# One PSUM pool for the whole program, exponential's table taken up early, and the first query copies on VectorE, in a perceiver layer on one core

## The chip, the cores and the metric

The kernel runs on one core of a Trainium2 chip. It is one launch. The metric is the time of the device in microseconds (us), the median of several runs. All data are float32. The engines are TensorE (PE), VectorE (DVE), ScalarE (ACT), GpSimd (POOL) and SyncE (SP), which here issues the loads and stores. Matrix products are written to PSUM, which has eight banks of 128 partitions by 512 float32 values; VectorE and ScalarE read them from there.

## What is computed

One layer of a perceiver with 256 query tokens of 512 channels and 25088 context tokens: cross attention with a sigmoid instead of a softmax, causal self-attention of 16 heads with one set of keys and values, and a mixture of 64 experts, 8 to a token, with a shared expert.

```python
def xattn(q, k, v, ...):                       # 256 x 512, 25088 x 512
    qp, kp, vp = q @ Wq.T + bq, k @ Wk.T + bk, v @ Wv.T + bv
    return sigmoid(qp @ kp.T / sqrt(128)) @ vp

def attn(x, ...):
    xn = layernorm(x, ln_g, ln_b)
    q, (k, v) = xn @ w_q.T, split(xn @ w_kv.T)       # 16 heads of 64; one k, one v
    p = softmax(causal(q * scale @ k.T))
    return layernorm((p @ v, all heads) @ w_out.T, lno_g, lno_b)

def ffn(x, ...):
    shared = (silu(g) * u) @ s_down * sigmoid(x @ shared_gate_w)
    w, idx = top_k(softmax(x @ gate_w), 8)           # of 64 experts
    return sum over the 8 of w * ((silu(g_e) * u_e) @ e_down) + shared

x = x + xattn(layernorm(x), context, context)
x = x + attn(layernorm(x))
x = x + ffn(layernorm(x))
```

## The kernel before

The program is one function, `tile_perceiver_layer`. `T` is 256 tokens in `NT` = 2 tiles of `P` = 128, `D` is 512 channels in `ND` = 4 chunks. Tiles of memory come from pools; a scheduler places the waits. An instruction waits for earlier users of the tiles that it touches, and a new tile in a used buffer waits for the readers of the old one. When a pool is closed and another takes its place, a tile in that place waits for the last users of the old pool there. Many instructions are given to `in_turn`, which keeps the written order among the instructions of an engine; the gate, up and down matmuls of the shared part and the experts (L899 to L965) are mostly not, so the scheduler moves them.

The cross stage (L448 to L485) goes over 49 groups of 512 context tokens. For each group the context is transposed, keys `pk` and scores `pz` are made, and the sigmoids `zT` are multiplied with the context. This last product is made by seven products of half size ("00", "01", "2", "3", "1", "4", "11", L427 to L446), which are added up in PSUM over all groups: they lie in four banks, `held` (L389), two products to a bank, from the pool `pacc`. The other four banks, the pool `psum`, are handed out in turn by `bank`. After the last group eight VectorE instructions (L491 to L498) combine the products to `zc`, which is transposed (`pt_zc`), multiplied with the value weights (`py`, L530) and normed (`an`, L541). The first tile of `an` is transposed during the second `py` (L539): ScalarE copies four chunks out of PSUM into `anT`.

Then `cross.close()` gives both pools back (L543) and the pool `psum_b` takes all eight banks (L545): one bank each for the tags `pa`, `po`, `pt0`, `pt1`, and two pairs for the scores (`ps2`). The self-attention's heads are worked on in `NE` = 8 pairs. For each pair: `queries` (four matmuls, L624, and a copy `aq` by ScalarE, L633), `scored` (L702: four matmuls, then VectorE adds the mask and takes the maxima), `exponential` (L731, ScalarE), `divided` (L745: VectorE's reciprocals, then POOL's product), `turned` (transposes `ptp` and copies `pT`) and `weighted` (`po`, L784). The loop (L798) staggers these: a round makes the scores of pair e, and turns the probabilities of pair e − 2; `queries` runs one or two pairs ahead. Queries of pairs 1 and 3 take the bank `po`, the others `pa`. Before the loop stand keys, values and queries of pair 0, in halves, as the tiles of `anT` come.

The output projection (`project`, L683) adds up `pw_0` and `pw_1` over the pairs. Some of its matmuls are fillers (L696) that the last rounds put between the others. `attended` norms the result, adds the residual (`x2`) and norms it again (`fn`).

At L852 the heads' pool is closed, and `pacc_b` (two banks) and `psum_c` (six banks) open. `route` (L863) makes the router's logits `pl`, `gate_up_products` the first shared products in two banks `first` (L931), before and after the second tile of `fn` is transposed. `run` (L967) then goes over four parts of the shared expert and eight whole experts: `gate_up` (two banks `ph`), and one step later `down` (L944), which makes the two token tiles `pd` one after the other in the two banks of `pacc_b`, each followed by VectorE's addition to `y` (L959, L963). Seven experts with few tokens are done by `few_*`, gathered in rounds; `few_spread` (L1213) adds them to `y` by `pd_few` in the banks of `pacc_b` too. SP loads each expert's weights (`load_expert`) when a buffer of the pool `wpool`, of three, is free.

Of the kernel before, what the change touches and what calls it, by code (L numbers as in the profile page):

```python
# [9 lines left out]
F32 = mybir.dt.float32  # L10
AF = mybir.ActivationFunctionType
ALU = mybir.AluOpType
AX = mybir.AxisListType

P = 128
# [6 lines left out]
def tile_perceiver_layer(  # L22
# [25 lines left out]
    nc = tc.nc  # L48

    T, D = x.shape  # L50
# [9 lines left out]
    ND = D // P  # L60
# [11 lines left out]

    cross = ExitStack()
    cpool = cross.enter_context(tc.tile_pool(name="cpool", bufs=2))
    psum = cross.enter_context(tc.tile_pool(name="psum", bufs=4, space=bass.MemoryType.PSUM))
    pacc = cross.enter_context(tc.tile_pool(name="pacc", bufs=4, space=bass.MemoryType.PSUM))

    def bank(name):
        return psum.tile([P, 512], F32, tag="ps", name=name)

    def accbank(name):
        return pacc.tile([P, 512], F32, tag="acc", name=name)

# [169 lines left out]
        in_turn(nc.vector.reciprocal(rs, sd))  # L255
        in_turn(nc.vector.tensor_scalar(dst, src, mean, rs, ALU.subtract, ALU.mult))

    def transposed_tile(dst, src, t, nm, by_act, g=None, b=None, psum_of=None):


        pt = bank(f"pt_{nm}_{t}") if psum_of is None else psum_of(f"pt_{nm}_{t}")
        for c in range(ND):
            in_turn(
                nc.tensor.transpose(
                    pt[:, c * P : (c + 1) * P], src[:, t, c * P : (c + 1) * P], ident
                )
            )
        pc = pt.rearrange("p (c q) -> p c q", c=ND)
        to = dst[:, :, t * P : (t + 1) * P]
        if g is None:  # L270
            if by_act > 0:
                in_turn(nc.scalar.copy(to[:, 0:by_act, :], pc[:, 0:by_act, :]))
            if by_act < ND:
                in_turn(nc.vector.tensor_copy(to[:, by_act:ND, :], pc[:, by_act:ND, :]))
            return
        for c in range(ND):
            if c < by_act:
                in_turn(
                    nc.scalar.activation(
                        to[:, c, :], pc[:, c, :], AF.Identity, bias=b[:, c : c + 1],  # L280
                        scale=g[:, c : c + 1],
                    )
                )
            else:
                in_turn(
                    nc.vector.tensor_scalar(
                        to[:, c, :], pc[:, c, :], g[:, c : c + 1], b[:, c : c + 1],
                        ALU.mult, ALU.add,
                    )
                )  # L290
# [95 lines left out]

    NP = J // 2
    HD = D // 2
    held = [accbank(f"xacc_{i}") for i in range(4)]  # L389
    product = {  # L390
        nm: held[i // 2][:, (i % 2) * HD : (i % 2 + 1) * HD]
        for i, nm in enumerate(("00", "01", "2", "3", "1", "4", "11"))
# [133 lines left out]
    for t in range(NT):  # L526
# [14 lines left out]
        layernorm(an[:, t, :], x1[:, t, :], f"a{t}", twice=True)  # L541

    cross.close()  # L543
    heads_psum = ExitStack()
    psum = heads_psum.enter_context(  # L545
        tc.tile_pool(name="psum_b", bufs=1, space=bass.MemoryType.PSUM)
    )

    def head_bank(tag, name):
        return psum.tile([P, 512], F32, tag=tag, name=name)  # L550

    def score_banks(name):
        return psum.tile([P, 2, 512], F32, tag="ps2", name=name, bufs=2)

# [57 lines left out]
    kk = hpool.tile([P, T], F32, tag="kk", name="kk")  # L616
    va = hpool.tile([P, NT, DH], F32, tag="va", name="va")

    def queries(e, lo=0, hi=T, tag="pa", mark=lambda ins: ins):

        pa = head_bank(tag, f"pa_{e}_{lo}")
        for c in range(ND):
            mark(
                nc.tensor.matmul(  # L624
                    pa[:, 0 : hi - lo],
                    lhsT=a_wqT_sb[:, c, e * P : (e + 1) * P],
                    rhs=anT[:, c, lo:hi],
                    start=(c == 0),
                    stop=(c == ND - 1),
                )  # L630
            )
        in_turn(
            nc.scalar.activation(aq[:, e, lo:hi], pa[:, 0 : hi - lo], AF.Copy, scale=1.0 / DH)  # L633
        )

    def head_keys(lo, hi):
        pkk = head_bank("po", f"pkk_{lo}")
        for c in range(ND):
            in_turn(
                nc.tensor.matmul(  # L640
                    pkk[:, 0 : hi - lo],
                    lhsT=a_wkv_sb[:, c, 0:2, :].rearrange("p i d -> p (i d)"),
                    rhs=anT[:, c, lo:hi],
                    start=(c == 0),
                    stop=(c == ND - 1),
                )
            )
        nc.scalar.copy(kk[:, lo:hi], pkk[:, 0 : hi - lo])

    def head_values(t):  # L650
        pv = head_bank("pt1", f"pv_{t}")
        for c in range(ND):
            in_turn(
                nc.tensor.matmul(
                    pv[:, :DH],
                    lhsT=anT[:, c, t * P : (t + 1) * P],
                    rhs=a_wkv_sb[:, c, 2, :],
                    start=(c == 0),
                    stop=(c == ND - 1),
                )  # L660
            )
        in_turn(nc.vector.tensor_copy(va[:, t, :], pv[:, :DH]))


    first_scores = score_banks("ps_0")
    head_keys(0, P)
    queries(0, 0, P, mark=in_turn)
    transposed_tile(
        anT, an, 1, "an", 2, ln_g_sb, ln_b_sb, lambda name: head_bank("pt0", name)
    )  # L670
    head_values(0)
    head_keys(P, T)
    queries(0, P, T, mark=in_turn)
    head_values(1)


# [5 lines left out]

    def project(t, e):  # L683
        if len(pw) == t:
            pw.append(head_bank("pa", "pw_0") if t == 0 else score_banks("pw_1")[:, 0, :])
        in_turn(
            nc.tensor.matmul(  # L687
                pw[t],
                lhsT=oT[:, e, t * P : (t + 1) * P],
                rhs=a_wout_sb[:, e, :],  # L690
                start=(e == 0),
                stop=(e == NE - 1),
            )
        )

    fillers = [(0, e) for e in range(NE - 1)] + [(1, 0)]  # L696

    def fill(n):
        for _ in range(n):
            project(*fillers.pop(0))  # L700

    def scored(e):  # L702

        ps = first_scores if e == 0 else score_banks(f"ps_{e}")
        parts = []
        for t in range(NT):
            nk = (t + 1) * P
# [44 lines left out]
    def turned(e):  # L752


        found = [pe for pe, _ in scores_of.pop(e)[2]]
        done = []
        for kt in range(NT):
            pt = head_bank(f"pt{kt}", f"ptp_{e}_{kt}")
            n = (NT - kt) * P
            for i in range(2):  # L760
                for t in range(kt, NT):
                    o = i * n + (t - kt) * P
                    in_turn(
                        nc.tensor.transpose(
                            pt[:, o : o + P], found[t][:, i, kt * P : (kt + 1) * P], ident
                        )
                    )
            pT = work_b.tile([P, 2, n], F32, tag=f"pT{kt}", name=f"pT_{e}_{kt}")
            to = pT.rearrange("p i q -> p (i q)")
            if kt == 0:  # L770
                in_turn(nc.vector.tensor_copy(to, pt[:, : 2 * n]))
            else:
                in_turn(nc.scalar.copy(to, pt[:, : 2 * n]))
            done.append(pT)
        return done

    def weighted(e, done):


        po = head_bank("po", f"po_{e}")  # L780
        for kt, pT in enumerate(done):
            for i in range(2):
                in_turn(
# [10 lines left out]


    scores_of = {}
    queries(1, tag="po", mark=in_turn)
    for e in range(NE + 2):  # L798
        done = None
        if e == 2:  # L800
            queries(e + 2, mark=in_turn)
        if e - 2 in scores_of:
            done = turned(e - 2)
        if e - 1 in scores_of:
            divided(e - 1, 0)
            divided(e - 1, 1)
        if e == 1:
            queries(e + 1, mark=in_turn)
        if e != 2 and 0 < e < NE - 2:
            queries(e + 2, tag="po" if e == 1 else "pa", mark=in_turn)  # L810
        if e >= NE - 2:
            fill(2 if e < NE else 1)
        if e < NE:
            scores_of[e] = scored(e)
        if done is not None:
# [26 lines left out]
    fill(len(fillers))  # L842
    project(0, NE - 1)
    attended(0)
    for e in range(1, NE):
        if e == NE - 1:
            transposed_tile(fT, fn, 0, "fn", ND, psum_of=lambda name: head_bank("pt0", name))
        project(1, e)
    attended(1)

    heads_end.close()
    heads_psum.close()  # L852
    pacc = ctx.enter_context(tc.tile_pool(name="pacc_b", bufs=2, space=bass.MemoryType.PSUM))
    psum = ctx.enter_context(tc.tile_pool(name="psum_c", bufs=6, space=bass.MemoryType.PSUM))
    few = ctx.enter_context(tc.tile_pool(name="few", bufs=1))


# [3 lines left out]
    pls = []  # L861

    def route(t):  # L863
        pl = bank(f"pl_{t}")
        for c in range(ND):
            in_turn(
                nc.tensor.matmul(
# [60 lines left out]

    first = [bank(f"ph_first_{half}") for half in range(2)]  # L931
    route(0)
    gate_up_products(("s", 0), first, 0, P, in_turn)
    transposed_tile(fT, fn, 1, "fn", 2)
# [9 lines left out]
    def down(n, hT):  # L944
        _, dn = weights.pop(n)
        nm = f"{n[0]}{n[1]}"
        for t in range(NT):
            pd = accbank(f"pd_{nm}_{t}")
            for f in range(NI):
                nc.tensor.matmul(  # L950
                    pd,
# [259 lines left out]
        nc.scalar.copy(of_sb[:, r, :], po)  # L1211

    def few_spread():  # L1213
        for t in range(NT):
            pd = accbank(f"pd_few_{t}")
            for r in range(NR):
                nc.tensor.matmul(  # L1217
                    pd,
# [126 lines left out]
```

## Time and profile before

| | us |
|---|---|
| median of 3 runs | 803.3 (802.87 to 804.76) |
| the profiled execution | 804.36 |
| its span | 802.6 |
| TensorE busy | 786.0 (98%) |
| VectorE busy | 496.0 (62%) |
| ScalarE busy | 112.3 (14%) |
| POOL busy | 19.3 (2%) |

The span runs from the first to the last instruction that the profile shows; the time of the execution has a little more around it. The page shows the span in 40 slices of 20 us. In tenths, 9 being 90% or more:

```profile
PE   8999999999999999999999999999999899999996
...
DVE  5766777667776677667776677766546453512212
ACT  2111100111011110111101110011145220110110
...
PEclk9999999999999999999999999999999999999999
DMA  9997999999999888988889888910600032769500
```

The cross stage ends at about 565 us, the heads run to about 640 us, the shared part and the experts to the end. The rows of DMA give the mean share of 16 DMA engines; PEclk is the clock that TensorE was granted, in tenths of the full one, as a mean of the slice.

### The profile page before, as it was taken

What the parts mean: (1) busy time and instruction counts of PE and PEld (TensorE: products, weight loads), DVE (VectorE), ACT (ScalarE), POOL (GpSimd) and SP (SyncE); (2) the same over time, 40 slices, a digit from 0 to 9 for tenths busy, and PEclk for the clock granted to TensorE, in tenths of its full rate; (3) what the DMA queues carried; (4) which work ended last, traced back from release to release, by engine and by line L of the source; (5) the groups of instructions that cost most, each with busy time, mean ns of one, the idle gap of its engine ahead of it and who ended that gap; (6) DMA issues with size and microseconds to landing.
All of it is one profiled execution on the core that took longest, in us unless ns stands there. A gap on an engine that the chain in (4) does not pass through costs nothing.

```text
span 802.6 us, 8728 instructions
## 1 busy us (share of the span) xinstructions
PE 786.0 (98%) x3310; PEld 565.8 (70%) x3310; DVE 496.0 (62%) x819; ACT 112.3 (14%) x248; POOL 19.3 (2%) x42
## 2 busy tenths in 40 slices
PE   8999999999999999999999999999999899999996
PEld 5777777777777777777777777777675576776563
DVE  5766777667776677667776677766546453512212
ACT  2111100111011110111101110011145220110110
POOL 1000000000000000000000000000123000000000
PEclk9999999999999999999999999999999999999999
DMA  9997999999999888988889888910600032769500
GB/s 251 242 198 182 266 237 256 241 228 227 216 205 197 188 180 176 203 189 192 177 179 207 187 188 171 190 53 0 228 10 1 1 131 83 249 222 386 187 1 30
DMA packets 150496, 139.59 MB, mean 174 GB/s; under 512 B 7984, under 2 KB 109872, under 8 KB 150448
## 3 DMA queue, kind: packets, MB, share of 16 engines
q1 hardware_dynamic: 150160, 138.96, 73.7%
q8 instruction: 28, 0.46, 0.3%
q14 instruction: 20, 0.16, 0.1%
q10 hardware_dynamic: 288, 0.00, 0.0%
HBM read 138.42 MB, written 0.52 MB: 173 GB/s over the span
## 4 chain that ended last, share of the span: by engine, by line
PE 95%; DVE 2%; ACT 1%; POOL 1%; DMA 0%; issue 0%; ACTq 0%; POOLq 0%; DVEq 0%
PE xacc L439 37%; PE pk L338 21%; PE pz L360 11%; PE ph_e L904 7%; PE pd_e L950 3%; PE ph_s L904 3%; PE pd_s L950 2%; PE pw L687 2%; PE pa L624 1%; PE ph_few L1172 1%; PE py L530 1%; PE ph_first L904 1%; PE po_few L1203 1%; PE ps L713 1%; PE pf L1149 1%; PE pd_few L1217 1%
## 5 line engine op out<-in xcount | busy, mean ns | idle before, releaser
L338 PE MATMUL pk<-cT,wkT_sb 128*128 128x512 f32 x376 | 169.0, 592 | 0.0
L439 PE MATMUL xacc<-T,S 128*128 128x256 f32 x588 | 134.9, 379 | 0.0
L368 ACT ACTIVATE zT<-pz 128x512 f32<-128x512 f32 x98 | 58.3, 597 | 479.9 <-PE pz L360 479.2
L439 PEld LDWEIGHTS xacc<-T,S 128*128 128x128 f32 x588 | 111.7, 190 | 15.2
L338 PEld LDWEIGHTS pk<-cT,wkT_sb 128*128 128x128 f32 x376 | 71.4, 190 | 69.9 <-issue 67.4
L309 DVE STREAM_TRANSPOSE cT<-quarters 128x2048 f32<-128x2048 f32 x47 | 108.2, 2303 | 0.0
L439 PEld LDWEIGHTS xacc<-ctx,zT 128*128 128x128 f32 x392 | 74.3, 190 | 31.3 <-issue 23.0
L439 PE MATMUL xacc<-ctx,zT 128*128 128x256 f32 x392 | 93.0, 380 | 0.1
L360 PE MATMUL pz<-qT,kT 128*128 128x256 f32 x392 | 92.6, 379 | 0.0
L360 PEld LDWEIGHTS pz<-qT,kT 128*128 128x128 f32 x392 | 74.4, 190 | 10.1
L407 DVE TENSOR_TENSOR S<-zT 128x256 f32<-128x256 f32 x49 | 20.8, 425 | 91.5 <-ACT zT L368 91.5
L347 DVE TENSOR_SCALAR kT<-pk,bk 128x512 f32<-128x512 f32 x49 | 36.8, 751 | 59.8 <-PE pk L338 59.8
L904 PE MATMUL ph_e<-fT,gu 128*128 128x256 f32 x256 | 57.2, 381 | 0.0
L380 DVE TENSOR_TENSOR zsum<-zsum,zT 128x1024 f32<-128x1024 f32 x48 | 56.8, 1182 | 0.0
L904 PEld LDWEIGHTS ph_e<-fT,gu 128*128 128x128 f32 x256 | 48.1, 190 | 10.6 <-issue 3.8
L439 PE MATMUL xacc<-T,zT 128*128 128x256 f32 x196 | 50.3, 379 | 0.0
L439 PE MATMUL xacc<-ctx,S 128*128 128x256 f32 x196 | 50.3, 379 | 0.0
L439 PEld LDWEIGHTS xacc<-T,zT 128*128 128x128 f32 x196 | 37.2, 190 | 5.1
L439 PEld LDWEIGHTS xacc<-ctx,S 128*128 128x128 f32 x196 | 37.2, 190 | 5.1
L418 DVE TENSOR_TENSOR T<-ctx,T 128x512 f32<-128x512 f32 x49 | 33.9, 692 | 1.7
L419 DVE TENSOR_TENSOR T<-ctx 128x512 f32<-128x512 f32 x49 | 33.5, 684 | 0.0
L420 DVE TENSOR_TENSOR T<-T,ctx 128x512 f32<-128x512 f32 x49 | 33.5, 683 | 0.0
(225 smaller groups left out, 611.3 us busy)
## 6 DMA issues: line engine op xcount, KB each, us to landing
ctx<-in_context SPq DMA_DIRECT2D x48, 1024.0 KB, 7.5
quarters<-in_context SPq DMA_DIRECT2D x188, 256.0 KB, 9.3
gu<-in_e_gate_up SPq DMA_DIRECT2D x12, 1024.0 KB, 7.8
dn<-in_e_down SPq DMA_DIRECT2D x11, 512.0 KB, 5.5
gu_s<-in_s_gate_up SPq DMA_DIRECT2D x8, 512.0 KB, 6.6
a_wqT<-in_a_wqT SPq DMA_DIRECT2D x1, 2048.0 KB, 9.0
a_wout<-in_a_woutT SPq DMA_DIRECT2D x1, 2048.0 KB, 9.0
dn_s<-in_s_down SPq DMA_DIRECT2D x4, 512.0 KB, 8.3
```

The source lines that it names most:

```text
L309: in_turn(nc.vector.transpose(cT, q.rearrange("p b (c r) -> p c b r", r=R)))
L338: nc.tensor.matmul(pk, lhsT=w[:, c, :], rhs=cT[:, c, :, :].rearrange("p b r -> p (b r)"), start=(c == 0), stop=(c == ND - 1),)
L347: in_turn(nc.vector.tensor_scalar(kT, pk, bk_sb, None, ALU.add))
L360: nc.tensor.matmul(pz[:, i * T : (i + 1) * T], lhsT=kT[:, j * P : (j + 1) * P], rhs=qT, start=True, stop=True,)
L368: nc.scalar.activation(zT[:, 2 * h : 2 * h + 2, :].rearrange("p j t -> p (j t)"), pz, AF.Sigmoid, scale=1.0 / math.sqrt(QK),)
L380: in_turn(nc.vector.tensor_add(zsum, zsum, zT))
L418: in_turn(nc.vector.tensor_sub(t2, c_of(ct, 1, 1), t1))
L419: in_turn(nc.vector.tensor_sub(t3, c_of(ct, 1, 1), c_of(ct, 0, 1)))
L420: in_turn(nc.vector.tensor_sub(t4, t2, c_of(ct, 1, 0)))
L439: nc.tensor.matmul(product[nm], lhsT=lhs[:, p, :], rhs=rhs[:, p, :], start=(g == 0 and p == 0 and nm in ("00", "2", "1", "11")), stop=(g = ...
L904: nc.tensor.matmul(ph[:, f * T + lo : f * T + hi], lhsT=gu[:, c, col : col + P], rhs=fT[:, c, lo:hi], start=(c == 0), stop=(c == ND - 1),)
L950: nc.tensor.matmul(pd, lhsT=hT[:, f, t * P : (t + 1) * P], rhs=dn[:, f, :], start=(f == 0), stop=(f == NI - 1),)
```

## The change

All three pools become one, `psum`, open from the start to the end, with eight banks: three of a tag "one", one of a tag "apart", and two pairs of a tag "two", each pair one tile.

- `bank` takes in turn three tiles of "one" and one of "apart".
- `held` is cut from two pairs. So are `first`, both halves of each `pd` and of `pd_few`, the scores `ps` and `pw_1`.
- `pkk`, `pv`, `ptp`, `po`, the transposes and `pl` take "one"; all `queries` and `pw_0` take "apart".
- A small exponential, `warm`, is put on ScalarE between the transposes of the second tile of `an` and the second values and keys.
- The copies `aq` of pairs 1 to 3 are made by VectorE, the others as before by ScalarE.
- There is one more filler, (1, 1), and the last round takes two of them.

```diff
-    psum = cross.enter_context(tc.tile_pool(name="psum", bufs=4, space=bass.MemoryType.PSUM))
-    pacc = cross.enter_context(tc.tile_pool(name="pacc", bufs=4, space=bass.MemoryType.PSUM))
+    psum = ctx.enter_context(tc.tile_pool(name="psum", bufs=3, space=bass.MemoryType.PSUM))
+    turns = [0]
 
     def bank(name):
-        return psum.tile([P, 512], F32, tag="ps", name=name)
-
-    def accbank(name):
-        return pacc.tile([P, 512], F32, tag="acc", name=name)
+        turns[0] += 1
+        return apart(name) if turns[0] % 4 == 0 else among_three(name)
+
+    def among_three(name):
+        return psum.tile([P, 512], F32, tag="one", name=name)
+
+    def apart(name):
+        return psum.tile([P, 512], F32, tag="apart", name=name, bufs=1)
+
+    def banks(name):
+        return psum.tile([P, 2, 512], F32, tag="two", name=name, bufs=2)
...
-    held = [accbank(f"xacc_{i}") for i in range(4)]
+    held = [pair[:, i, :] for pair in (banks("xacc_0"), banks("xacc_1")) for i in range(2)]
...
-    heads_psum = ExitStack()
-    psum = heads_psum.enter_context(
-        tc.tile_pool(name="psum_b", bufs=1, space=bass.MemoryType.PSUM)
-    )
...
-    def queries(e, lo=0, hi=T, tag="pa", mark=lambda ins: ins):
-
-        pa = head_bank(tag, f"pa_{e}_{lo}")
+    def queries(e, lo=0, hi=T):
+
+        pa = apart(f"pa_{e}_{lo}")
...
-        in_turn(
-            nc.scalar.activation(aq[:, e, lo:hi], pa[:, 0 : hi - lo], AF.Copy, scale=1.0 / DH)
-        )
+        to, src = aq[:, e, lo:hi], pa[:, 0 : hi - lo]
+        if 0 < e < 4:
+            in_turn(nc.vector.tensor_scalar(to, src, 1.0 / DH, None, ALU.mult))
+        else:
+            in_turn(nc.scalar.activation(to, src, AF.Copy, scale=1.0 / DH))
...
     head_keys(0, P)
-    queries(0, 0, P, mark=in_turn)
-    transposed_tile(
-        anT, an, 1, "an", 2, ln_g_sb, ln_b_sb, lambda name: head_bank("pt0", name)
-    )
+    queries(0, 0, P)
+    transposed_tile(anT, an, 1, "an", 2, ln_g_sb, ln_b_sb)
+
+    warm = small.tile([P, 1], F32, tag="warm", name="warm", bufs=1)
+    in_turn(nc.scalar.activation(warm, eps_sb, AF.Exp))
     head_values(0)
...
-    fillers = [(0, e) for e in range(NE - 1)] + [(1, 0)]
+    fillers = [(0, e) for e in range(NE - 1)] + [(1, 0), (1, 1)]
...
-            fill(2 if e < NE else 1)
+            fill(2)
...
-    for e in range(1, NE):
+    for e in range(2, NE):
...
-    heads_psum.close()
-    pacc = ctx.enter_context(tc.tile_pool(name="pacc_b", bufs=2, space=bass.MemoryType.PSUM))
-    psum = ctx.enter_context(tc.tile_pool(name="psum_c", bufs=6, space=bass.MemoryType.PSUM))
...
-    first = [bank(f"ph_first_{half}") for half in range(2)]
+    pair = banks("ph_first")
+    first = [pair[:, half, :] for half in range(2)]
...
+        pair = banks(f"pd_{nm}")
         for t in range(NT):
-            pd = accbank(f"pd_{nm}_{t}")
+            pd = pair[:, t, :]
...
     def few_spread():
+        pair = banks("pd_few")
         for t in range(NT):
-            pd = accbank(f"pd_few_{t}")
+            pd = pair[:, t, :]
```

## The prediction

> **What bounds the kernel now.** I read the busy shares and the chain of waits first. TensorE (PE) is busy for 98% of the span and makes up 95% of the chain that ended last, so the time is TensorE's work plus the few gaps on it; work moved between other engines counts only where it opens or closes such a gap.
>
> ```profile
> PE 786.0 (98%) x3310; PEld 565.8 (70%) x3310; DVE 496.0 (62%) x819; ACT 112.3 (14%) x248; POOL 19.3 (2%) x42
> ...
> PE 95%; DVE 2%; ACT 1%; POOL 1%; DMA 0%; issue 0%; ACTq 0%; POOLq 0%; DVEq 0%
> ```
>
> Next the table of TensorE's waits. Columns: total, times, longest, in us. Four of these stand where the change works.
>
> ```profile
> PE pl L867 <- DVE rs_o L834: 1.9, 1, 1.9
> PE pkk L640 <- POOL xb L680: 1.6, 1, 1.6
> ...
> PE pa L624 <- ACT aq L633: 0.9, 1, 0.9
> PE po L784 <- ACT pT L773: 0.7, 1, 0.7
> ```
>
> Then the timeline (start, length, engine, line; in brackets the idle time before and what ended it) at the three places that the change touches: the end of the cross stage,
>
> ```profile
> 562.08 1.03 PE L439 MATMUL xacc<-ctx,S 128*128 128x256 f32 x4
> 562.94 1.03 PE L439 MATMUL xacc<-T,zT 128*128 128x256 f32 x4
> 563.14 0.42 DVE L495 TENSOR_TENSOR u<-u,xacc 128x256 f32<-128x256 f32 x1 [0.61 <-PE xacc L439]
> ...
> 564.37 0.85 PE L297 MATMUL pt_zc<-ident,zc 128*128 128x128 f32 x6 [0.18 <-DVE zc L497]
> ```
>
> the start of the heads,
>
> ```profile
> 576.39 1.50 ACT L279 ACTIVATE anT<-pt_an,ln_b,ln_g 128x128 f32<-128x128 f32 x4 [1.91 <-PE pt_an L264]
> ...
> 577.99 1.13 PE L640 MATMUL pkk<-anT,a_wkv 128*128 128x128 f32 x8 [1.64 <-POOL xb L680]
> ...
> 589.05 1.28 ACT L738 ACT_TABLE_LOAD   x1 [2.51 <-DVE nmx L727]
> ...
> 592.10 0.17 DVE L749 RECIPROCAL rsm<-sums 128x2 f32<-128x2 f32 x1 [0.74 <-ACT pe L738]
> ...
> 592.39 1.99 PE L624 MATMUL pa<-anT,a_wqT 128*128 128x256 f32 x8 [0.91 <-ACT aq L633]
> ```
>
> and the end, where each half of the last expert's sum is read while TensorE works on:
>
> ```profile
> 792.63 3.60 PE L950 MATMUL pd_e<-dn,hT_e 128*128 128x512 f32 x8
> ...
> 794.55 0.75 DVE L963 SCALAR_TENSOR_TENSOR y<-pd_e,wso,y 128x512 f32<-128x512 f32 x1 [1.03 <-PE pd_e L950]
> ```
>
> **A. The accumulators become pairs (+0.86).** Until the end of the cross stage the instructions and what they wait for are the same on every engine: the rotation of three tiles and one reproduces that of four. Then `held` is two tiles of two banks each, and a wait follows the tile, not the bank. L495 reads product "1", which is in the second pair, so it waits for the last matmul into that pair, "11", which ends at 562.94 + 1.03 = 563.97; before, it waited for "4", ending 562.08 + 1.03 = 563.11, and started at 563.14. So it and the `zc` pieces behind it start 563.97 − 563.11 = 0.86 later. The first copy waits for "3" too, but ends long before that. The transposes `pt_zc` stand behind `zc` and nothing fills TensorE: +0.86. Bounds: 0 (if waits went by bank) and 0.86 + 0.42, one more read.
>
> **B. The start of the heads (+1.49).** Three things. First, `pkk` no longer waits for a whole pool to be given back. The waits table names POOL's `xb`, which happens to end then but touches nothing of `pkk`; the four copies of `anT` on ScalarE end at 576.39 + 1.50 = 577.89, 0.1 before `pkk` starts, and they are the last readers of the old pool. Now each matmul waits for its own copy only: the copies and the 1.13 of matmuls overlap, and `pa_0` starts at 578.23 instead of 578.96: −0.73, kept up to the first scores, since the second half of `an` (DVE, 578.31 + 0.55) is ready just in time.
>
> Second, the table load of 1.28 leaves the path: it is done while ScalarE waits for TensorE. The first exponential starts when the maxima are there, 589.05 − 0.73 = 588.32, instead of 590.35.
>
> Third, and against these, all `queries` share the one bank `apart` (before, heads 2 and 3 had two), and the copy that frees it is on VectorE for heads 1 to 3. In VectorE's order the copy of `pa_2` stands behind the two reciprocals of head 0 (L749). The second of these waits for the last exponential of head 0: in before 592.10 − 590.35 = 1.75 after the first one, so now 588.32 + 1.75 = 590.07. The reciprocal takes 0.17, the copy about 0.48 (the like of `qT`, 128x256 out of PSUM, L467), so the bank is free at 590.75 and `pa_3` starts at 590.85. TensorE ends `pa_2` at 588.0. A new stall of 2.85, which nothing fills: behind `pa_3` in TensorE's order are `ps_1`, `pa_4` and the first turned probabilities. `ps_1` comes at 592.68 instead of 590.55. The old wait of `pa_4` (0.91) and some of that of `po` (0.7) go, since ScalarE's copies no longer queue behind the exponentials: `ps_2` is at 596.11 instead of 594.97 and `pa_5` at 599.46 instead of 597.97. So +1.49, and from there heads follow at the same pace. Bounds: −2.13 if the copy were not behind the reciprocals (−0.73, −0.91, −0.49), +2.85 − 0.73 = +2.12 if none of the later waits shrank.
>
> **C. The end of the heads (−1.84).** `pl` (L867) waited for the old pool's last reader, `rs_o` on VectorE, 1.88; now it needs only `fT`, written by 634.83. The filler (1,1), moved ahead, is a matmul of 0.86 that fills waits before the last `po`; `fn` is sooner by 0.19. So `pl` starts at 634.74 instead of 636.95, and the sixteen matmuls behind it (L904) end at 639.28. Then the second `pt_fn` needs the second `fn`, which VectorE ends at 639.17 + 0.55 − 0.19 = 639.53: it starts at 639.65, not 641.49, so the chain of VectorE gives 1.84 of the 2.21. Bounds: −2.21 and −1.09, the latter if the layer norm were behind another DVE instruction of 0.75.
>
> **D. The shared part and the experts (+0.35).** A `pd` is a pair now, so its second half waits until VectorE has read the first: 0.2 from the matmul's end to the read, 0.75 for the read, 0.1 back, 1.05. In the new order eleven of the thirteen pairs have at least three gate matmuls (0.44 each) or two `pd` matmuls (0.86 each) between their halves, 1.3 to 1.7, so it is hidden there; where VectorE comes late, some 0.1 to 0.25 shows at two places. Bounds 0 and 1.0. The weights of experts 3 and 8 are asked for up to 7.5 later on SP's queue, as their buffers come free later; by SP's rows they landed 7 to 10 before their use, which hides it; what it costs without that lead is rival 3.
>
> **E. The end (+1.21).** `pd_few` has one matmul (0.86) between its halves against 1.05: about +0.15. The last `pd_e` has none: TensorE stands still for the whole 1.05, and the last addition and the store follow. +1.21 in all; bounds 0 and 2.1.
>
> **The sum** is 0.86 + 1.49 − 1.84 + 0.35 + 1.21 = +2.07 of TensorE time.
>
> **The clock** comes on top. TensorE was granted half its clock once inside the kernel. Columns of the windows: busy time and instructions of PE, PEld, DVE, ACT and POOL, then the granted clock.
>
> ```profile
> 564.00:567.63 3.63, 3.37 (x26) 2.73 (x25) 2.20 (x8) 0.00 (x0) 0.00 (x0) 1.00 0.02 5
> 567.63:571.05 3.42, 3.42 (x6) 1.34 (x5) 1.34 (x2) 0.00 (x0) 0.00 (x0) 0.50 0.75 251
> ```
>
> A spell of 3.42 at 0.50 costs 3.42/2 = 1.7 of work, and it followed 3.6 us in which TensorE is shown busy, but with transposes and single-column sums. So less than a full idle stretch is enough. A stall of 2.85 within one such stretch leaves at most 0.6 of work in it, so a new spell at `pa_3` is likely, at 0 to 1.7; taken at 1.1, about two chances in three, because where the stretch begins is not known. The stall of 1.88 at `pl` brought no spell in this execution.
>
> The Trainium skill ("TensorE: Matmul & The Clock Gate", Part 1) has the half rate follow an idle window of about 3.4 us, and its table of advice warns of gaps of over 3 us. By that rule alone the stall at `pa_3` is short enough and the sum stays +2.07; the row above shows the gate to be stricter than the rule, so the row decides.
> The Trainium skill ("ScalarE: Activation LUTs", What ACT_TABLE_LOAD costs) gives some 2.66 us for a switch of tables, drain included. The trace shows 1.28, and the exponential starts 0.02 after it; by the page the move would spare 1.4 more, and `pa_3` would come no sooner, as its wait is worked out from the maxima.
>
> **The forecast**: +2.07 + 1.1 = +3.2. The sum is made against the profiled execution (804.36, of it 802.6 the span), which is 1.1 over the median of the runs, 803.3; on the median 803.3 + 3.2 = 806.5. Without a spell it is 805.4, with one in full 807.1.
>
> **Rivals.** (1) Not slower: VectorE's copy of `pa_2` does not hold TensorE, because the bank comes free before the reciprocals are due. For it: VectorE is idle 2.21 before the first of them (its row of 591.18). Then B is −2.13, the sum 0.86 − 2.13 − 1.84 + 0.35 + 1.21 = −1.55, and there is no new spell: 801.7; with A at its 0 and C at its −2.21, 800.5. Against it: the copy's place in the order, if VectorE takes its instructions in turn, as its rows of before do. It decides as soon as the copy runs before some 590. Chance 0.16. (2) The two cancel: the pair waits are smaller than the rows say (E 0.3, D 0) and no spell comes: 0.86 + 1.49 − 1.84 + 0.3 = +0.8, 804.1. For it: past the first 10 us none of TensorE's gaps of over 1 us in before was followed by a spell; the one spell came without such a gap. Chance 0.16. (3) Much slower: the weights that SP asks for later eat their lead, and an expert waits. Price: 7.5 − 7 = 0.5, and the transfer of one expert's 1.5 MB at the 386 GB/s of the busiest slice, 3.9: +4.4 on the forecast, 810.9. It decides once the lead of 7 is gone. For it: these loads land in that slice, 720 to 740. Against it: the lead of the others is up to 10. Chance 0.06.
>
> **How the numbers follow.** My forecast has 0.62; its own range is 804.8 to 808. A measurement of this kernel can hardly tell less than 0.3% (2.4 us, so 800.9 to 805.7) from no change. Of the forecast's chance, 0.12 lies below 805.7 (no spell, small D) and 0.50 above; rival 2 lies in the band, rival 3 above it, and rival 1 lies half under 800.9 and half in the band, between its 800.5 and 801.7. Faster 0.08, same 0.08 + 0.16 + 0.12 = 0.36, slower 0.50 + 0.06 = 0.56. The range 801.4 to 808.6 leaves out about half of rival 1, rival 3 and a little above the forecast's own range, some 0.17.
>
> **What would show it.** A: L495's successor starts on the end of "11". B: `pkk` without its 1.6 wait, no table load before the first exponential, and a wait of nearly 2.9 of `pa` on VectorE's `aq`, perhaps with half a clock behind it. C: no wait of `pl` on `rs_o`. E: a wait of 1 us of the last `pd_e` on VectorE's `y`. It is wrong if `pa_3` follows `pa_2` at once, or if the waits of `pd` are many.

## The result, and the profile after

The changed kernel took 808.46 us in the median of five runs (807.09 to 810.35), the kernel before 804.62 (802.87 to 806.1) in five: slower by the ratio 1.0056, with a 95% interval of 1.0032 to 1.008, which is some 4.5 us. (That is the difference of the means, 808.83 and 804.33; the medians differ by 3.84.) Two executions of other runs, one of before at 837.7 and one of `no_warm` at 1395.85, were in a slower state, at mean granted clocks of 0.945 and 0.557, and are left out of every comparison. The profiled execution of the changed kernel was its fastest, 807.09, with a span of 805.2.

TensorE still makes up the chain that ended last: from its page, the busy shares and the chain,

```profile
PE 788.5 (98%) x3310; PEld 566.5 (70%) x3310; DVE 497.7 (62%) x822; ACT 111.5 (14%) x246; POOL 19.4 (2%) x42
...
PE 94%; DVE 3%; DMA 1%; ACT 1%; POOL 1%; issue 0%; SPq 0%; ACTq 0%; POOLq 0%; DVEq 0%
```

and TensorE's waits (total, times, longest). The waits of `pl` on `rs_o`, 1.9, and of `pkk` on the old pool, 1.6 with the table's wrong name for it, are gone or down to 0.6. Three new ones stand in their place:

```profile
PE pa L621 <- DVE aq L631: 2.5, 1, 2.5
...
PE pt_zc L306 <- DVE zc L506: 1.1, 1, 1.1
...
PE pd_e L947 <- DVE y L960: 0.8, 1, 0.8
PE pkk L639 <- ACT anT L288: 0.6, 1, 0.6
```

The timeline of the changed kernel at the end of the cross stage, at the start and the end of the heads and at the end of the kernel. The first row is the first read of the second pair, after its last product (563.26 + 1.03); the row of 590.50 is `pa_3`, behind VectorE's copy, behind the second reciprocal:

```profile
564.33 0.42 DVE L504 TENSOR_TENSOR u<-u,xacc 128x256 f32<-128x256 f32 x1 [0.80 <-PE xacc L448]
...
565.56 0.85 PE L306 MATMUL pt_zc<-ident,zc 128*128 128x128 f32 x6 [1.05 <-DVE zc L506]
...
566.82 1.95 PE L515 MATMUL pr<-ones_sb,zsum 128*128 128x1 f32 x16 [0.41 <-DVE zcT L309]
...
580.45 1.28 ACT L668 ACT_TABLE_LOAD   x1
...
588.21 0.37 ACT L736 ACTIVATE pe<-ps,nmx 128x128 f32<-128x128 f32 x1 [5.26 <-DVE nmx L725]
...
589.96 0.17 DVE L747 RECIPROCAL rsm<-sums 128x2 f32<-128x2 f32 x1 [0.75 <-ACT pe L736]
590.04 0.40 DVE L631 TENSOR_SCALAR aq<-pa 128x256 f32<-128x256 f32 x1
...
590.50 3.68 PE L621 MATMUL pa<-anT,a_wqT 128*128 128x256 f32 x8 [2.47 <-DVE aq L631]
...
637.90 1.08 PE L862 MATMUL pl<-gates,fT 128*128 128x65 f32 x8
...
642.86 0.63 PE L273 MATMUL pt_fn<-ident,fn 128*128 128x128 f32 x4 [0.25 <-DVE lg L871]
...
797.01 1.98 PE L947 MATMUL pd_e<-dn,hT_e 128*128 128x512 f32 x4 [0.84 <-DVE y L960]
799.03 0.75 DVE L960 SCALAR_TENSOR_TENSOR y<-pd_e,wso,y 128x512 f32<-128x512 f32 x1 [2.08 <-PE pd_e L947]
```

`pa_3` itself takes 3.68 where `pa` takes 1.89 to 1.99 elsewhere. The windows (busy time and instructions of five engines, then the granted clock) tell why:

```profile
587.20:590.66 3.46, 0.99 (x5) 0.54 (x4) 1.57 (x5) 1.72 (x8) 1.07 (x2) 0.99 0.00 0
590.66:594.07 3.41, 3.41 (x8) 2.27 (x8) 0.00 (x0) 0.00 (x0) 0.58 (x1) 0.50 0.02 5
```

Half the clock for 3.41 us, right after a stretch in which TensorE had 0.99 of work. In this execution the `py` stage, where before's profile had its spell, ran at full clock.

Start times of the same work in the two profiles give the balance of the stages:

| start of | before | after | difference |
|---|---|---|---|
| last product "11" | 562.94 | 563.26 | +0.32 |
| second part of `pt_zc` | 564.37 | 565.56 | +1.19 |
| `pr` | 565.30 | 566.82 | +1.52 |
| first `pt_an`, behind `py` | 575.75 | 575.57 | −0.18 |
| `pa_0` | 578.96 | 578.09 | −0.87 |
| `ps_1` | 590.55 | 594.11 | +3.56 |
| `ps_3` | 599.79 | 602.93 | +3.14 |
| first `pl` | 636.95 | 637.90 | +0.95 |
| second `pt_fn` | 641.49 | 642.86 | +1.37 |
| last addition to `y` | 796.27 | 799.03 | +2.76 |

One spell of half clock is in each column, at `py` in before (10.45 from `pr` to `pt_an`, 8.75 in after) and at `pa_3` in after (3.68 − 1.89 = 1.79).

### The profile page after: what moved, and what is told of

It reads as the page before. It is cut to its first block, busy times and chain, and to the rows that moved or that the text cites. A ratio compares the mean times of both kernels' runs of the same rounds, so it can differ in the third digit from the quotient of the medians.

```text
span 805.2 us, 8713 instructions
## 1 busy us (share of the span) xinstructions
PE 788.5 (98%) x3310; PEld 566.5 (70%) x3310; DVE 497.7 (62%) x822; ACT 111.5 (14%) x246; POOL 19.4 (2%) x42
## 4 chain that ended last, share of the span: by engine, by line
PE 94%; DVE 3%; DMA 1%; ACT 1%; POOL 1%; issue 0%; SPq 0%; ACTq 0%; POOLq 0%; DVEq 0%
PE xacc L448 37%; PE pk L347 21%; PE pz L369 11%; PE ph_e L899 7%; PE pd_e L947 3%; PE ph_s L899 3%; PE pa L621 2%; PE pd_s L947 2%; PE ph_few L1169 1%; PE pw L685 1%; PE ps L711 1%; DMA gu_s<-in_s_gate_up 1%; PE pd_few L1215 1%; PE po_few L1200 1%; PE pf L1146 1%; PE ptp L762 1%
```

## The experiments

Two things had to be told apart: how much each new wait costs, and how much the clock costs that follows the waits. My theory was that the three new waits (the pair of accumulators, the one bank for queries with its copy behind the softmax, the pair at the end) cost work and that the first two also bring half-clock spells. The rivals stand with each run. Every execution has its mean granted clock; a spell of 3.4 us lowers it by 0.002, and the times of a kernel fall into groups about 1.6 us apart that go with it. From these groups come the counts of spells; in every kernel of the table the profiled execution has as many spells as its group says:

| kernel | median | executions with 0, 1, 2, 3 spells | time at none | at one |
|---|---|---|---|---|
| before, in `before_again` and beside the others | 803.2 to 804.7 | 35, 39, 12, 0 | 802.9 | 804.6 |
| changed | 808.46 | 0, 1, 2, 2 | | 807.1 |
| `copy_first` | 805.12 | 1, 8, 3, 0 | 803.6 | 805.1 |
| `two_banks` | 804.98 | 2, 4, 6, 0 | 802.7 | 804.2 |
| `fill_stall` | 807.16 | 0, 4, 2, 0 | | 807.0 |
| `acc_single` | 806.12 | 0, 8, 4, 0 | | 805.8 |
| `last_single` | 807.39 | 0, 2, 3, 3 | | 805.7 |
| `by_act` | 808.17 | 0, 0, 5, 1 | | |
| `fill_zc` | 808.67 | 0, 2, 4, 0 | | 806.8 |
| `all_three` | 801.88 | 4, 7, 0, 0 | 800.4 | 802.1 |
| `all_three_act` | 801.97 | 2, 8, 0, 0 | 800.5 | 802.0 |
| `all_three_cold` | 803.06 | 5, 5, 2, 0 | 801.5 | 803.2 |

**The kernel before again.** No edit.

> The kernel before, run five times more so that the mean granted clock of each execution is seen beside its time. Theory: part of the slowdown is half-clock spells of TensorE, 3.4 us each (mean clock lower by 0.002), and the changed kernel has about two in an execution (its five clocks were 0.996, 0.994, 0.995, 0.992, 0.993) where before has about one. Then the clocks here are mostly 0.996 to 0.998, none under 0.994, and the median lies at 803 to 805 us. Rival, the clock has no part in it: clocks here spread over 0.992 to 0.996 as well.

Twelve executions: 802.68 to 803.12 at clocks of 0.998 and 0.999 (three), 804.6 to 804.84 at 0.996 and 0.997 (six), 806.03 to 806.72 at 0.995 (three). The profile of one at 802.89 has no half clock before its work ends. So the clock differs from run to run in one and the same kernel, and before has 0.7 spells in the mean of all its runs, the changed kernel 2.2. The rival falls; so does the belief that 803.3 was the middle of before's runs: it lies near its level without a spell.

**The copy ahead of the reciprocals.**

```diff
-        if e - 1 in scores_of:
-            divided(e - 1, 0)
-            divided(e - 1, 1)
         if e == 1:
             queries(e + 1)
+        if e - 1 in scores_of:
+            divided(e - 1, 0)
+            divided(e - 1, 1)
```

> The changed kernel with VectorE's copy of pa_2 ahead of the two reciprocals of head pair 0; one bank for all queries stays. Theory (the stall of 2.5 at pa_3 comes from the place of the copy in VectorE's order): the wait falls to about 0.6 (the maxima end 588.1, the copy of 0.4 ends 588.5, pa_2 ended 588.0), ps_2 is 1.9 sooner, no half clock follows there, so 1.9 plus about 1.1 to 1.7 of clock: 805 to 805.8 on 808.5. Rival (one bank is the cause, whatever the order): the wait stays over 1.5 and the time over 807.5.

Measured 805.12, and in its table of waits

```profile
PE pa L621 <- DVE aq L631: 0.5, 1, 0.5
```

in place of 2.5. With one spell in each it is 805.1 against 807.1, so 2.0 is work, and the mean of spells falls from 2.2 to 1.2. The place of the copy makes the stall; one bank alone leaves 0.5 of it.

**A second bank for pair 3.**

```diff
-        pa = apart(f"pa_{e}_{lo}")
+        pa = among_three(f"pa_{e}_{lo}") if e == 3 else apart(f"pa_{e}_{lo}")
```

> The changed kernel with pa_3 in a bank of the three, not the one apart; VectorE's copy of pa_2 stays behind the reciprocals. Theory (the stall needs both, the one bank and the copy's place): pa_3 follows pa_2 at once, the copy at 590.0 is in time for pa_4, no half clock there: 2.0 to 2.5 less work and about one spell less, median 804.6 to 805.2, lowest 803.0 to 803.6. Rival (the reciprocals hold the copy and this holds pa_4 or ps_2 instead): the wait shows at pa_4, 807 and more.

`pa` has no wait in the table any more, though the copy stays where it was. Median 804.98; 802.7 without a spell, somewhat under what I expected, 804.2 with one, 2.9 less than the changed kernel. The stall needs both, the one bank and the late copy.

**The copies back on ScalarE.**

```diff
-        if 0 < e < 4:
+        if False:
```

> The changed kernel with the copies aq of pairs 1 to 3 on ScalarE as before; one bank for all queries stays. Theory (one bank and a copy queued behind the softmax of pair 0, on whichever engine): ScalarE ends its four exponentials at about 589.9, then copies pa_2 in 0.4, so pa_3 still waits 2.3 to 2.5 and the time is that of the changed kernel: one spell 807, median 807 to 809. Rival (VectorE as the copier is the fault): the wait is under 1 and the median near 805.

`pa` waits 2.2 for ScalarE's `aq` instead of 2.5 for VectorE's, and the median is 808.17 (ratio to before 1.0054, 1.0038 to 1.0069): the copier is not the cause. ScalarE's four exponentials end when VectorE's reciprocals can start, so a copy behind either comes equally late.

**Idle matmuls in the stall.**

```diff
+        if e == 1:
+            pi = among_three("pi_gap")
+            for _ in range(2):
+                in_turn(nc.tensor.matmul(pi, lhsT=a_wout_sb[:, 0, 0:P], rhs=a_wout_sb[:, 0, :], start=True, stop=True))
         if e != 2 and 0 < e < NE - 2:
             queries(e + 2)
```

> The changed kernel with two idle matmuls of 512 columns (0.86 each) between pa_2 and pa_3, in the stall of 2.5, results not used. Nothing is computed sooner. Theory (the stall brings a half-clock spell): about 0.8 of wait is left, pa_3 starts as late as before, but at full clock (1.9 instead of 3.7), and the median falls by 1.0 to 1.7 to about 807. Rival (the spells come from elsewhere or cost nothing): 808 to 809.

Median 807.16. Two rows of its timeline:

```profile
589.47 1.88 PE L811 MATMUL pi_gap<-a_wout 128*128 128x512 f32 x4
592.10 1.99 PE L621 MATMUL pa<-anT,a_wqT 128*128 128x256 f32 x8 [0.75 <-DVE aq L631]
```

(`pa_3` starts at 592.10 here, not 590.50, because this execution had its one spell before, in the `py` stage.) Nothing is computed sooner, but `pa_3` now takes 1.99, not 3.68, and no execution of six has three spells. At one spell it is as long as the changed kernel, 807.0. This is the stall's clock by itself: about 0.9 of a spell in the mean, 1.3 us in the median.

**The accumulators in single banks.**

```diff
-    def banks(name):
-        return psum.tile([P, 2, 512], F32, tag="two", name=name, bufs=2)
+    pacc = cross.enter_context(tc.tile_pool(name="pacc", bufs=4, space=bass.MemoryType.PSUM))
...
-    held = [pair[:, i, :] for pair in (banks("xacc_0"), banks("xacc_1")) for i in range(2)]
+    held = [pacc.tile([P, 512], F32, tag="acc", name=f"xacc_{i}") for i in range(4)]
...
     cross.close()
+    pairs = ctx.enter_context(tc.tile_pool(name="pairs", bufs=2, space=bass.MemoryType.PSUM))
+
+    def banks(name):
+        return pairs.tile([P, 2, 512], F32, tag="two", name=name)
```

> The changed kernel with the four accumulators of the cross stage in four single banks of a pool of their own, closed after that stage; the pairs open in its place. Theory (the pair makes L504 wait for the last product of the pair): pt_zc's wait of 1.1 falls to about 0.2, pr's of 0.4 to under 0.1, so 1.2 less at a like number of half-clock spells (807.1 falls to 805.9 with one spell), and with less idle time ahead of py the spells there get no more: median 806 to 807.3. Rival (the wait is shifted to the values product, which waits for zcT anyway): no change, 808 to 808.8.

In its timeline the transposes wait as little as in before:

```profile
564.42 0.85 PE L305 MATMUL pt_zc<-ident,zc 128*128 128x128 f32 x6 [0.18 <-DVE zc L505]
```

Median 806.12; at one spell 805.8 against 807.1, 1.3 less. Its rows account for 0.88 of that: `pr` starts 2.68 after the last product, against 3.56 in the changed kernel and 2.36 in before. The wait of `pr` stayed at 0.4, against what I expected. Spells fall to 1.3 in the mean, from 2.2.

**An idle matmul in that wait.**

```diff
+    pi = among_three("pi_zc")
+    in_turn(nc.tensor.matmul(pi, lhsT=wvT_sb[:, 0, 0:P], rhs=wvT_sb[:, 0, :], start=True, stop=True))
     transposed(zcT, zc, "zc")
```

> The changed kernel with one idle matmul of 512 columns (0.86) in TensorE's wait of 1.05 for zc at the end of the cross stage, result not used. Theory (the longer wait there makes half-clock spells in the py stage more frequent): nothing starts sooner, the times with one spell stay at 807, but spells fall from about two in an execution to 1.2 to 1.5, median 807 to 807.5. Rival (spells in the py stage come from the transposes and single-column sums alone): still two in the mean, median 808 to 808.7.

A miss: the median is 808.67. Two executions of six have one spell, four have two, 1.7 in the mean, between what the two theories expect. With so few runs it decides nothing by itself. It also leaves `pr`'s wait of 0.4 and moves two transposes behind the idle matmul. That the longer wait makes spells in the `py` stage more frequent is shown by the others: of kernels without a stall at `pa_3`, those with the wait of 1.05 (`copy_first`, `two_banks`, `fill_stall`, 30 executions) have 1.3 spells in the mean, those without it (`all_three` and `all_three_act`, 21) have 0.7. The traces, cut along the clock's own stretches in the last section, show the same and how it comes about.

**The end in single banks.**

```diff
-            pd = pair[:, t, :]
+            pd = bank("pd_last") if t == 1 and n == ("e", WHOLE - 1) else pair[:, t, :]
...
-            pd = pair[:, t, :]
+            pd = bank("pd_few_1") if t == 1 else pair[:, t, :]
```

> The changed kernel with the second half of the last expert's down product, and of the sum over the few-token experts, in a bank of its own (the rotation of single banks is idle there). Theory (a pair is one tile, so the second half waits for the read of the first): the wait of pd_e on y of 0.84 goes, and the last addition is 1.2 to 1.3 sooner: 807.2. Rival (the tail is hidden behind the store of the first half): same as the changed kernel, 808.5, though the wait is gone.

Median 807.39; at one spell 805.7 against 807.1, so 1.4 of work, and the spells stay as many (2.1). The wait of `pd_e` is gone from the table. The store does not hide it.

**Without the early table.**

```diff
-    warm = small.tile([P, 1], F32, tag="warm", name="warm", bufs=1)
-    in_turn(nc.scalar.activation(warm, eps_sb, AF.Exp))
```

> The changed kernel without the early exponential. Theory (the table load of 1.28 is then on the path to the first exponential and so to pa_3): the wait at pa_3 grows from 2.5 to 3.8, lowest 808.3 and median 809.7 to 811. By the notes' 2.66 for a switch it would grow by 2.7, median 811 and more. Rival (the load is hidden while VectorE takes the maxima): same as the changed kernel, 808.5.

Median 810.15, lowest 809.38, of five; its executions have two or three spells, in groups too near each other for the table above. Its waits and its timeline:

```profile
PE pa L621 <- DVE aq L631: 3.7, 1, 3.7
```

```profile
589.73 1.28 ACT L734 ACT_TABLE_LOAD   x1 [5.24 <-DVE nmx L723]
591.02 0.37 ACT L734 ACTIVATE pe<-ps,nmx 128x128 f32<-128x128 f32 x1
```

The wait grows from 2.47 to 3.75, by the 1.28 of the load and no more; the exponential follows it by 0.01. The Trainium skill's 2.66 for a switch ("ScalarE: Activation LUTs", What ACT_TABLE_LOAD costs) does not show here: ScalarE had been idle for 5.24, so if a drain is part of a switch, it cost nothing.

**All three new waits away**: `two_banks`, `acc_single` and `last_single` in one.

> The changed kernel with all three of its new waits taken away: accumulators in four single banks, pa_3 in a second bank, the last product's and the few-token sum's second half in a bank of their own. What it keeps is the one pool at the two borders and the early table. Theory (the effects add up): with no spell the changed kernel is at about 805.5; less 1.2, 2.2 and 1.3 it is at 800.8, with at most one spell in the mean: median 801 to 802.6, under before's 803.2 to 804.6. Rival (they overlap, since VectorE's chain then sets the end of each stage): 803 or more.

Median 801.88, ratio to before 0.9966 (0.9955 to 0.9977): faster than both. At one spell in each, the three single gains sum to 1.3 + 2.9 + 1.4 = 5.6, and together they are 807.1 − 802.1 = 5.0. Apart from the accumulators it keeps the one pool where stages meet, and it keeps the early table: 802.9 − 800.4 = 2.5 less work than before.

**Its copies on ScalarE, and it without the early table.**

> The version without the three new waits (800.4 without a spell, 802.0 with one), with the copies of pairs 1 to 3 by ScalarE. Theory (with two banks the copier does not matter, since pa_3 needs none of them): 800.2 to 800.9 without a spell, 801.8 to 802.5 with one. Rival (the copies crowd the exponentials on ScalarE, as in before, where pa_4 waited 0.9): 801.3 without a spell.

> The version without the three new waits, without the early exponential. Theory (the load of 1.28 then delays the exponentials, and behind them the copy that pa_4 waits for): pa_4 waits 0.5 to 1.0, and 0.6 to 1.3 more in all: 801.0 to 801.7 without a spell. Rival (slack in the heads takes it): 800.4 without a spell, as with it.

With the copies on ScalarE 801.97, 800.5 without a spell: the same. Without the table 803.06, 801.5 without a spell, so the early table is worth 1.0 there; `pa` waits 1.2, a little over what I expected.

## Why the prediction was right and wrong

It said slower and named the waits; 806.5 was forecast, 808.46 came. Point by point:

- A, +0.86: `pt_zc` came 1.19 − 0.32 = 0.87 later. The `pr` behind it lost 0.33 more, which I had not seen. In before it starts when the first of VectorE's four copies `zcT` has ended (565.24, `pr` at 565.30), in after only when the second has (566.76, `pr` at 566.82). This is not the pairs' doing: without them, in `acc_single`, `pr` waits for the second copy too. It came with the rest of the new pool, though the prediction took its rotation of three banks and one to act like that of four; which part of it, no run shows.
- B, +1.49: from −0.18 to +3.14 is 3.32, less the spell of 1.79 is 1.53. Its parts hold too: −0.69 at `pa_0` for −0.73, 2.47 of stall for 2.85 (the copy took 0.40, not 0.48, and began before the reciprocal was done). `copy_first`, `two_banks` and `by_act` show that it was for the reason given. The first rival, that the bank is free before the reciprocals are due, fell: the copy ran at 590.04.
- C, −1.84: from +3.14, which the heads keep, to +1.37, −1.77. The one pool does what it says, and VectorE's chain takes the rest of what `pl` gained.
- D, +0.35: under 0.1. From the second `pt_fn` on, the gate products of the shared part and the experts start 1.34 to 1.46 later where the order is the same, and one down product of 1.72 later still where that was pulled ahead of them. Other matmuls cover nearly every read of a pair. Weights asked for later did not show, so the third rival fell. The second rival had D right, but not E and not the clock.
- E, +1.21: 2.76 − 1.46 = 1.30.

The sum of work was +2.07 by the prediction and 1.20 + 1.53 − 1.77 + 0.09 + 1.30 = +2.35 by the traces. The step that failed is the clock, "a new spell at `pa_3` is likely, at 0 to 1.7; taken at 1.1". The runs show 2.2 spells in the changed kernel (2.1 and 2.2 in `last_single` and `by_act`, which keep both waits) against 0.7 in before, 1.5 more at about 1.6 each, 2.4 us in place of the 1.1. I had counted one place and priced it by its chance. But the stall at `pa_3` brings about one spell in nearly every execution (0.9 by `copy_first`, `two_banks` and `fill_stall`; in the traces, all six of kernels with the stall have half clock right behind it, and none of the eight others there), and the wait of A, for which I had counted its idle time alone, adds half a spell or more in the `py` stage (0.6 from `all_three` to the kernels that have the wait, 0.9 by `acc_single`). The second failure is the base: I put the sum on 803.3, the middle of three runs, which is before's level without a spell, while the profiled execution, 804.36, had one. On the five-run median of 804.62 my +3.2 would have been 807.8.

So 2.35 + 2.4 = 4.7, near the 4.5 of the measured ratio.

The Trainium skill ("TensorE: Matmul & The Clock Gate", Part 1) has the clock halved after an idle window of about 3.4 us. No idle stretch of these kernels comes near that except 3.75 in `no_warm`; the half clock came after 2.47 of idle with 0.99 of work in the stretch, and in the `py` stage after waits of 1.05 or less among transposes and single-column sums. The rows decided rightly against the rule. Its sentence that the window runs freely fits the groups of times, since the same program gets none, one or two spells, and the traces: the clock first rises 4.43 to 7.34 us after the first instruction, elsewhere in each.

## What to carry to other kernels

When banks are joined into one tile to save a pool, look at the last use of each joined tile in its stage: a wait follows the tile, and where nothing stands behind it in TensorE's order, it costs the read in full. A copy that frees a bank belongs ahead of any instruction that waits for a longer chain, on whichever engine it is, or the bank needs a second. A TensorE-bound kernel can pay for a gap twice, as time and as clock: the 2.2 to 3.75 at `pa_3` were followed by half clock in all six traces that have them, the 1.64 of `pkk` and the 1.88 of `pl` in neither trace of before. So such a gap is priced by the work that is left in the 3.41 us around it and by the share of executions that it throws into half clock, and the base of a forecast needs enough runs to know which of these levels it is.

## What the runs showed of the hardware

The granted clock changes on a fixed grid. In each of the fourteen traces every later change of it within the span lies a whole number of times 3.413 us behind its first rise. The half clock lasts one such stretch, or two on end in `copy_first` and `two_banks`, although TensorE is shown busy throughout the first of the two. The windows of `copy_first` in its `py` stage, cut along the grid:

```profile
564.90:568.31 3.41, 2.25 (x19) 2.04 (x19) 2.36 (x7) 0.00 (x0) 0.00 (x0) 1.00 0.02 5
568.31:571.73 3.42, 3.42 (x8) 1.94 (x9) 1.57 (x3) 0.00 (x0) 0.00 (x0) 0.50 0.38 118
571.73:575.14 3.41, 3.41 (x5) 1.35 (x4) 0.00 (x0) 0.00 (x0) 0.00 (x0) 0.50 1.05 347
```

What decides is the work in the stretch before, if it is counted in this way: TensorE's busy time without the single-column sums (`pr`), and half of it where the stretch itself ran at half clock. The fourteen traces hold 3240 such stretches between the first rise and TensorE's last matmul. All 16 with at most 1.40 us were followed by half clock, and none of the other 3224, the lowest of which has 1.41.

| stretch | shown busy | counted | next at half clock |
|---|---|---|---|
| after, 587.21, the stall at `pa_3` | 0.95 | 0.95 | yes |
| before, 564.22, with all of `pr` | 3.18 | 1.37 | yes |
| `copy_first`, 564.90 | 2.25 | 0.85 | yes |
| `copy_first`, 568.31, at half clock, `pr` up to 569.10 | 3.41 | 1.31 | yes |
| `fill_zc`, 564.94 | 2.91 | 1.40 | yes |
| `fill_zc`, 568.35, at half clock | 3.41 | 1.41 | no |
| before, 567.63, at half clock, `py` alone | 3.41 | 1.71 | no |
| before, 574.46 | 1.89 | 1.89 | no |

With the sums counted in full, or with the transposes left out too, the two kinds overlap. This way of counting was found from the traces after all the runs, and no run tested it; the ends of matmuls in a profile are modelled, so the limit of some 1.4 in 3.41 is an estimate.

Where the grid falls differs from one execution to the next, and that is why one program has a spell in its `py` stage or none. The longer wait ahead of it widens the range that brings one. Of seven traces with the wait of 1.05, the five whose first rise is at 4.49 to 6.42 have the spell, and the two at 6.95 and 7.34 do not. Of six without it, those at 4.43 and 5.80 have the spell, and the four at 5.88 to 6.84 do not; in `fill_zc`, with an idle matmul in the wait, the first rise is at 5.15, and it has one.
